# First MLP's loads behind the projections' weights, the output projection's behind the fifth pair's; the third block's statistics pinned

## The chip, the cores and the metric

The kernel runs on one core of a Trainium2 chip. The metric is the device time in microseconds of one launch; three runs of the kernel before gave 1535.03, 1537.14 and 1538.2, median 1537.14. One further execution was recorded by the hardware profiler: 1529.18 us, of which the instructions span 1527.5. All durations below are of that execution.

A core has five engines, each with an instruction queue of its own that it works off strictly in order: PE (TensorE, matrix products), DVE (VectorE), ACT (ScalarE), POOL (GpSimd) and SP (SyncE). SP issues nearly all loads of this kernel; ACT issues some stores. An instruction whose inputs aren't ready holds up everything behind it on its engine. A load is done some microseconds after its issue, and the same 16 DMA engines carry the loads of all issuers.

## The reference

One sequence of 2048 tokens with 512 features goes through a normalisation, a Mamba2 mixer with a gated MLP, another normalisation and a routed mixture of experts. Cut to what matters here:

```python
x = x + attn(layernorm(x))
x = x + ffn(layernorm(x))

def attn(hidden):
    h = hidden + mamba2(rmsnorm(hidden, ln1_w))
    h2 = rmsnorm(h, ln2_w)
    return h + (silu(h2 @ gate_w) * (h2 @ up_w)) @ down_w

def mamba2(x):
    z, xb, B, C, dt = split(x @ in_proj_w)         # 512 -> 2576
    xb, B, C = split(silu(conv(xb, B, C)))
    y = ssd_chunked(xb * softplus(dt + dt_bias), dt * A, B, C) + D * xb
    return rmsnorm(y * silu(z), norm_w) @ out_proj_w   # 1024 -> 512

def ffn(x):                                        # 8 experts, best 2 of each token
    w = top2(softmax(x @ Wr))
    return sum(w[e] * ((silu(x @ Wg[e]) * (x @ Wu[e])) @ Wd[e]))
```

All arithmetic is in float32.

## The kernel before

**Blocks.** The Mamba2 part works in eight blocks (b) of 256 tokens, each of two chunks of 128 tokens (t = 2b + j). The MLP works in four blocks (fb) of 512 tokens, that is two Mamba2 blocks, and in 16 chunks (c) of the 2048 inner features. The MLP of a block runs spread out between the Mamba2 steps of later blocks: `main` steps both generators in turn, the first MLP from within block 2 on. After all of it come routing and experts, which the change doesn't touch.

**The input projection.** Its weights are ten pairs of 512 KB (pairs 0 to 5: x, B and C; 6 to 9: the gate z), reloaded for each block. `load_w_in` (L96) loads one pair into a tile `wi` of a ring of three; the load of pair p + 2 is issued as pair p begins (`projected`, from L330). The products are `pm` (L340, for x, B and C; `pm_0` to `pm_5`) and `pz` (the gate, in the same function). Block 0's six pairs are projected in `main` ahead of everything else; those of block b + 1 and the gates of block b run between the pieces of chunk work of block b.

**Normalisation.** `prepare(b)` (L209) makes a block's statistics (`scales`, L190: bn_stats L149, bn_aggr L150, a square root on ACT, a reciprocal on DVE), the normalised rows `hn` (L219, one per chunk), and their transposes for the projection (PE L201, `hT` written by DVE L205). For block 1 an existing `issue_after` keeps it behind block 0's rows.

**Chunk work.** ACT, POOL and DVE make a chunk's decays: per-row sums of time steps are written out and read back spread over all partitions (`spread`, L305: loads `cum` of 512 KB each at L312, masked by POOL at L314; `ec` at L324), exponentiated by ACT (L420) and multiplied by DVE (L422). `xd` (L428) is the chunk's x times its time steps; PE's state product (L452) takes it. `dA` (L270) comes out of the time-step chain of a block, and PE's `pc` (L273) begins the block's sums with it. At a chunk's end the output product `po` (L490) multiplies the gated rows `zs` by the output projection `w_o` (1024 x 512, 2048 KB, loaded once at L878). Before that POOL multiplies the eight row groups of `w_o` by the norm's weights, in place (`weigh`, L888), during block 0.

**The MLP's products.** Instead of eight products of quarter blocks for gate and up together, a chunk does seven, with sums of weights and of activations. In the first MLP (fb = 0) the weights come as blocks (`load_early` L524: three loads of 128 KB into `mg`; `load_late` L537: one of 256 KB into `ms`) and POOL makes the sums (L531, L532, L542, L543); ACT then issues the stores of the finished tiles to memory (L544, L545), and later MLPs load those. `mg` and `ms` share a ring of three tiles. `load_down` (L550) loads a chunk's 256 KB of the down projection into `md`, a ring of four. PE's products of gate and up are at L780, their copies out of PSUM on ACT at L827, L834 and L821, and the gate product on POOL at L847.

**What sets the order.** A scheduler that weighs the program's instructions puts each engine's queue in order when the kernel is built. An instruction that nothing holds can land far ahead of its place in the program: the first MLP's loads, which only need free tiles, stand near the start of SP's queue, and the third block's first bn_stats near the start of DVE's. `tc.issue_after(x)` makes the instructions inside it come behind instruction x in that order. From block 2 on PE's order is fixed by the program; the other engines' is the scheduler's throughout. The order is the same in each execution.

Of the kernel before, what the change touches and what calls it, by code (L numbers as in the profile page):

```python
# [16 lines left out]
P = 128  # L17
# [37 lines left out]
def mamba_mlp_moe(ctx, tc, x, w_in, w_out, w_gu, w_down, par, wr, wr_rows, wg, wu, wd, out):  # L55
# [3 lines left out]
    nc = tc.nc  # L59
# [33 lines left out]
    w_in_k = w_in.rearrange("(k p) n -> p k n", p=P)  # L93
    nc.sync.dma_start(out=w_dt, in_=w_in_k[:, :, 2560:2576])

    def load_w_in(pair):  # L96

        w = pw.tile([P, NK, 2 * P], F32, name="wi", tag="wi", bufs=3)
        nc.sync.dma_start(out=w, in_=w_in_k[:, :, pair * 2 * P : (pair + 1) * 2 * P])
        return w  # L100

    ahead = [load_w_in(pair) for pair in range(2)]
# [102 lines left out]
            nc.vector.tensor_tensor(dst, pt, bc(weight, 2, P), ALU.mult)  # L205

    first_rows = None

    def prepare(b):  # L209

        nonlocal first_rows
        hT = wa.tile([P, NK, TB], F32, name=f"hT{b}", tag="hT")
        hns = []
        with tc.issue_after(first_rows) if b == 1 else ExitStack():
            scales(b)
            for j in range(NCH):
                t = b * NCH + j
                hns.append(wa.tile([P, D], F32, name=f"hn{t}", tag="tok", bufs=3))
                normed = nc.vector.tensor_scalar(  # L219
                    hns[j], res[t], mv[:, t, 0:1], rboth[:, t : t + 1], ALU.subtract, ALU.mult  # L220
                )
# [49 lines left out]
        n = NCH * NH  # L271
# [123 lines left out]
    def chunk(b, j, dt, ncum, dtdec, cd, cum, ec, xb, cs, zs):  # L395

        nonlocal summed
        t = b * NCH + j
        tok = slice(j * P, (j + 1) * P)
        halves = [slice(half * HD, (half + 1) * HD) for half in range(2)]  # L400
        sdt = sdiag[t % 2]
        xbt = xbts.pop(t)
        y = zs[:, :, tok]

        for gp in range(2):

            if t:
                with tc.issue_after(summed), tc.high_priority(AT_ONCE):
                    nc.gpsimd.tensor_tensor(ec[:, gp], ec[:, gp], cs[gp][:, :, tok], ALU.mult)

            psc = ps_sg.tile([P, 2, 4, P], F32, name=f"psc{t}_{gp}", tag="sg")
            for half in range(2):
                rows = halves[half]
                nc.tensor.matmul(psc[:, half], xb[rows, 2 + gp, tok], cs[gp][rows, :, tok], start=True, stop=True)  # L414


            lt = cum[gp].rearrange("p (a i) q -> p a i q", a=2)
            turns = [(half, i, 8 * gp + 4 * half + i) for i in range(4) for half in range(2)]
            for half, i, h in turns:
                nc.scalar.activation(lt[:, half, i], lt[:, half, i], AF.Exp, bias=ncum[:, j, h : h + 1])  # L420
            for half, i, h in turns:
                nc.vector.scalar_tensor_tensor(  # L422
                    lt[:, half, i], lt[:, half, i], dt[:, j, h : h + 1], psc[:, half, i], ALU.mult, ALU.mult
                )
            if gp == 0 and t < NT - 1:

                xd = wa.tile([P, 4, 4, HD], F32, name=f"xd{t}", tag="xd", bufs=1)
                nc.vector.tensor_tensor(  # L428
                    xd, bc(xbt[:, 0], 2, 4),
                    bc(dtdec[:, j, :].rearrange("p (g i) -> p g i", g=4), 3, HD), ALU.mult,  # L430
                )
            if gp:
                yield
            py = ps_y.tile([P, 4, P], F32, name=f"py{t}_{gp}", tag="y")
            if t:
                for i in range(4):
                    nc.tensor.matmul(
                        py[:, i, :], sdt[:, gp, i, :], ec[:, gp, i, :], start=(i == 0), stop=False,
                        skip_group_check=True,
                    )  # L440
            yield
            if gp == 0:
                yield
            for half in range(2):
                nc.tensor.matmul(
                    py[halves[half]], xbt[:, 0, 2 * gp + half, :], lt[:, half], start=not t, stop=True,
                    skip_group_check=True,
                )
            if gp == 0 and t < NT - 1:
                pst = ps_tr.tile([P, 2, 4, HD], F32, name=f"pst{t}", tag="tr")  # L450
                for g in range(4):
                    nc.tensor.matmul(pst[halves[g % 2], g // 2], xbt[:, 1, g, :], xd[:, g], start=True, stop=True)  # L452


            yd = wa.tile([P, 4, P], F32, name=f"yd{t}_{gp}", tag="y")
            for i in range(4):
                at = C_D + 4 * gp + i
                nc.vector.scalar_tensor_tensor(
                    yd[:, i, :], xb[:, gp, tok], params[:, at : at + 1], py[:, i, :], ALU.mult, ALU.add
                )  # L460
            nc.vector.tensor_tensor(y[:, 4 * gp : 4 * gp + 4, :], yd, y[:, 4 * gp : 4 * gp + 4, :], ALU.mult)

        if t < NT - 1:
            new = state
            if t:
                flat = state.rearrange("p g i d -> p (g i) d")
                nc.gpsimd.tensor_tensor(flat, flat, bc(cd[:, j].rearrange("p g i -> p (g i)"), 2, HD), ALU.mult)
                nc.vector.tensor_tensor(state, state, pst, ALU.add)
            else:
                nc.vector.tensor_copy(state, pst)  # L470
            nxt = sdiag[(t + 1) % 2]
            for half in range(2):
                nc.scalar.copy(nxt[halves[half], :, :, half * HD : (half + 1) * HD], new[halves[half]])

        yield
        if t < NT - 1:
            xbts[t + 1] = turned_x(t + 1, xb if j == 0 else xc[0])

        sq = wa.tile([P, 8, P], F32, name=f"sq{t}", tag="xd", bufs=1)
        with tc.high_priority(AT_ONCE):  # L480
            nc.scalar.activation(sq[:, 0:4, :], y[:, 0:4, :], AF.Square)
            nc.scalar.activation(sq[:, 4:8, :], y[:, 4:8, :], AF.Square)
            for n in (4, 2, 1):
                summed = nc.gpsimd.tensor_tensor(sq[:, 0:n, :], sq[:, 0:n, :], sq[:, n : 2 * n, :], ALU.add).ins
        yield


        po = ps_y.tile([P, D], F32, name=f"po{t}", tag="y") if t >= BPF * NCH else bank("g", [D], f"po{t}")
        for m in range(8):
            nc.tensor.matmul(po, y[:, m, :], w_o[:, m, :], start=(m == 0), stop=(m == 7))  # L490
        yield
        pms = ps_tr.tile([P, 1], F32, name=f"pms{t}", tag="tr")
        nc.tensor.matmul(pms, sq[:, 0, :], ones[:, 0:1], start=True, stop=True)

        ry = wa.tile([P, 1], F32, name=f"ry{t}", tag="ry")
        rsqrt_eps(ry, pms, scale=1.0 / DI)
        h = wa.tile([P, D], F32, name=f"h{t}", tag="tok", bufs=3)
        nc.vector.tensor_scalar(h, res[t], mv[:, t, 0:1], rstd[:, t : t + 1], ALU.subtract, ALU.mult)
        nc.vector.scalar_tensor_tensor(h, po, ry, h, ALU.mult, ALU.add)
        nc.gpsimd.tensor_tensor(res[t], res[t], h, ALU.add)  # L500
        nc.scalar.dma_start(out=resd[t], in_=res[t])

        m2 = wa.tile([P, 1], F32, name=f"m2{t}", tag="m2")
        nc.scalar.activation(sq[:, 4:8, :].rearrange("p a q -> p (a q)"), h, AF.Square, accum_out=m2)
        r2 = wa.tile([P, 1], F32, name=f"r2{t}", tag="r2")
        rsqrt_eps(r2, m2, scale=1.0 / D)
        nc.vector.tensor_scalar_mul(h, h, r2)
        yield
        fb, off = divmod(t * P, FB)
        if off == 0:  # L510
            h2T[fb] = (wk if fb % 2 else wa).tile([P, 2, NK, FH], F32, name=f"h2T{fb}", tag="h2T", bufs=1)
        half, off = divmod(off, FH)
        transposed(h, h2T[fb][:, half, :, off : off + P], params[:, C_L2 : C_L2 + NK])
# [36 lines left out]
    def load_down(c):  # L550
        d = pmlp.tile([P, D], F32, name="md", tag="md", bufs=4)
        nc.sync.dma_start(out=d, in_=w_down[c * FC : (c + 1) * FC, :])
        return d
# [213 lines left out]
    def feed_forward(fb):  # L767

        nonlocal mlp_w, newest, turning
        if fb == 0:  # L770
            w = load_early(0, 0)
            mlp_w = w, load_late(0, 0, w)
        b11, b21, b22, t1, t2, t3, t4 = sums(fb)
        rows = []
# [13 lines left out]
        for c in range(NFC):  # L788
# [59 lines left out]
            if pair:  # L848
                mlp_down(fb, rows, 2 * (c % 2) + 1, pair)
            newest = a.rearrange("p h q -> p (h q)")  # L850
            made[c] = newest, load_down(c)
            if more:
                early, late = coming
            yield
# [15 lines left out]
    ready = None  # L870
    for pair in range(6):
        finish(project(0, pair, hT, *xc))
        if pair < 2:
            next(coming)
        elif pair == 2:
            ready = finish(coming)
            near = [spread(0, 0, ready[-1])]
    nc.sync.dma_start(out=w_o, in_=w_out.rearrange("(t p) n -> p t n", p=P))  # L878
    near.append(spread(0, 1, ready[-1]))
    xbts[0] = turned_x(0, xc[0])  # L880

# [390 lines left out]
```

## Time and profile before

| | |
|---|---|
| Runs | 1535.03, 1537.14, 1538.2 us |
| Profiled execution / its span | 1529.18 / 1527.5 us |
| Granted PE clock, mean | 0.994 |
| PE, DVE, ACT, POOL busy | 97%, 53%, 47%, 28% |
| First loads of `mg`, `ms`, `md` issued | 11.29 to 23.82 us |
| `w_o` issued | 6.52 us |
| Third to fifth `wi` issued | 5.27, 15.31, 20.97 us |
| Sixth and seventh `wi` issued (one entry) | 27.59 us |
| First `pm_5` matmul | 34.48 us |
| First use of `w_o` (POOL, L888) | 57.74 us |
| First output product begins / ends | 71.48 / 80.29 us |
| First MLP product on PE | 222.15 us |

Such a profile is read from the busiest engine: with PE at 97%, a stretch in which PE waits counts, and a busier DVE or ACT counts only where PE waits for it. For every group of instructions the page gives busy time, the mean length of one in nanoseconds, and after the second bar the time in which the engine stood idle just before, with what ended the wait. A float32 matmul is recorded as two, so the sixteen records of `pm` that stand together are one pair. The timeline gives the start of each run of equal instructions and, in brackets, the idle time ahead of it. The windows give the granted clock of PE, where 1.00 is full speed.

### The profile page before, as it was taken

The numbers are of one execution on the slowest core, as the hardware profiler recorded it, in microseconds if no ns is written. First come the engines' busy times: TensorE is split into PE (matmuls) and PEld (weight loads), VectorE is DVE, ScalarE is ACT, GpSimd is POOL, SyncE is SP. The second block draws the span as 40 slices with busy tenths as digits, with TensorE's granted clock in tenths as the row PEclk, the third lists the DMA queues.
The fourth block names the chain that finished last, engine by engine and source line by source line (L and its number), as shares of the span: only waits on it lengthen the run. The fifth ranks groups of instructions, "written<-read, shape, count | busy, mean of one in ns | idle before, by whom it ended". The sixth has DMA issues, their size and how long they took to land. (4 is left out here: it accounts for less than half of the span.)

```text
span 1527.5 us, 18831 instructions
## 1 busy us (share of the span) xinstructions
PE 1483.2 (97%) x6009; PEld 1006.8 (66%) x6009; DVE 812.5 (53%) x2119; ACT 723.7 (47%) x1309; POOL 430.5 (28%) x537
## 2 busy tenths in 40 slices
PE   8899999999999999999999999998999999999996
PEld 7656577677667676767676667665776666656653
DVE  7776875645555565657645764555343445322221
ACT  5887966735663578458745653232221122111110
POOL 3442324423242212121233121113121123533321
PEclk9999999999999999999999999999999999999998
DMA  9443445644554655656347554438879643443332
GB/s 306 133 145 118 145 135 184 197 145 162 165 177 149 224 167 176 192 166 210 125 105 246 173 168 139 165 121 206 270 222 253 202 116 67 55 75 69 63 62 36
DMA packets 138899, 238.00 MB, mean 156 GB/s; under 512 B 13744, under 2 KB 74032, under 8 KB 138800
## 3 DMA queue, kind: packets, MB, share of 16 engines
q1 hardware_dynamic: 116032, 186.79, 40.1%
q0 software_dynamic: 9088, 18.91, 7.3%
q10 hardware_dynamic: 13680, 31.07, 5.4%
q8 instruction: 51, 0.84, 0.2%
q14 instruction: 48, 0.39, 0.1%
HBM read 195.93 MB, written 40.80 MB: 155 GB/s over the span
## 5 line engine op out<-in xcount | busy, mean ns | idle before, releaser
L764 PE MATMUL pd<-md,a 128*128 128x512 f32 x512 | 238.8, 593 | 1.4 <-DVE r L765 0.9
L340 PE MATMUL pm<-hT,wi 128*128 128x256 f32 x768 | 185.3, 386 | 3.4 <-DMA wi<-in_w_in 3.4
L340 PEld LDWEIGHTS pm<-hT,wi 128*128 128x128 f32 x768 | 141.9, 192 | 28.6 <-issue 10.8
L765 DVE TENSOR_TENSOR r<-r,pd 128x512 f32<-128x512 f32 x128 | 87.5, 684 | 136.0 <-PE pd L764 132.7
L764 PEld LDWEIGHTS pd<-md,a 128*128 128x128 f32 x512 | 97.2, 190 | 76.4 <-issue 64.6
L361 DVE SCALAR_TENSOR_TENSOR ca<-pre,params,ca 128x256 f32<-128x256 f32 x288 | 141.7, 549 | 0.3
L780 PE MATMUL py<-h2T,ms 128*128 128x256 f32 x512 | 131.7, 380 | 2.0 <-DMA ms<-late 2.0
L340 PE MATMUL pz<-hT,wi 128*128 128x256 f32 x512 | 117.0, 381 | 0.0
L490 PE MATMUL po<-w_o,zs 128*128 128x512 f32 x256 | 114.5, 600 | 0.0
L847 POOL TENSOR_TENSOR a<-a,up 128x256 f32<-128x256 f32 x64 | 48.1, 752 | 230.3 <-DVE up L841 184.6
L1121 PE MATMUL epg<-ew,xgT 128*128 x288 | 109.0, 460 | 0.2 <-ACT xgT L203 0.2
L1121 PE MATMUL epu<-ew,xgT 128*128 x288 | 108.7, 459 | 0.0
L780 PEld LDWEIGHTS py<-h2T,ms 128*128 128x128 f32 x512 | 95.5, 190 | 17.8 <-issue 2.9
L340 PEld LDWEIGHTS pz<-hT,wi 128*128 128x128 f32 x512 | 94.9, 190 | 13.7 <-issue 0.8
L1143 PE MATMUL epd<-ew,ehT 128*128 (+1 forms) x216 | 99.0, 594 | 1.0 <-DVE ehT L1136 1.0
L420 ACT ACT_TABLE_LOAD x68 | 87.2, 1283 | 22.8 <-DMA xnd<-xn 8.4
L420 ACT ACTIVATE cum<-cum,ncum 128x128 f32<-128x128 f32 x256 | 84.6, 391 | 7.3 <-POOL cum L314 6.3
L490 PEld LDWEIGHTS po<-w_o,zs 128*128 128x128 f32 x256 | 49.1, 193 | 57.8 <-issue 56.5
L827 ACT COPY a<-px 128x256 f32<-128x256 f32 x64 | 23.6, 369 | 127.0 <-PE px L780 115.6
L1101 POOL DMA_INDIRECT xg<-xnd,idx x36 | 35.5, 985 | 157.7 <-PE pt L201 150.8
L314 POOL TENSOR_SCALAR_AFFINE_SELECT cum<-cum 128x1024 f32<-128x1024 f32 x32 | 36.2, 1131 | 151.0 <-DMA cum<-rowsd 140.7
L422 DVE SCALAR_TENSOR_TENSOR cum<-cum,dt,psc 128x128 f32<-128x128 f32 x256 | 72.2, 339 | 5.1 <-PE psc L414 2.8
(247 smaller groups left out, 2550.7 us busy)
## 6 DMA issues: line engine op xcount, KB each, us to landing
wi<-in_w_in SPq DMA_DIRECT2D x80, 512.0 KB, 3.9
ms<-late SPq DMA_DIRECT2D x48, 512.0 KB, 4.4
mg<-early SPq DMA_DIRECT2D x48, 384.0 KB, 3.9
md<-in_w_down SPq DMA_DIRECT2D x64, 256.0 KB, 4.3
cum<-rowsd SPq DMA_DIRECT2D x32, 512.0 KB, 4.3
col<-in_wr_rows SPq DMA_DIRECT2D x64, 256.0 KB, 3.9
late<-ms ACTq DMA_DIRECT2D x16, 512.0 KB, 2.6
ec<-rowsd SPq DMA_DIRECT2D x60, 128.0 KB, 4.0
```

Source lines behind the costliest of these rows:

```text
L314: nc.gpsimd.affine_select(out=c, in_=c, pattern=[[0, 8], [1, P]], compare_op=ALU.is_ge, fill=-3.0e38, base=0, channel_multiplier=-1,)
L340: nc.tensor.matmul(pm[:, m, :], w[:, k, m * P : (m + 1) * P], hT[:, k, :], start=(k == 0), stop=(k == NK - 1))
L361: nc.vector.scalar_tensor_tensor(ca, pre[:, m, k : k + TB], cw[:, k : k + 1], ca, ALU.mult, ALU.add)
L420: nc.scalar.activation(lt[:, half, i], lt[:, half, i], AF.Exp, bias=ncum[:, j, h : h + 1])
L422: nc.vector.scalar_tensor_tensor(lt[:, half, i], lt[:, half, i], dt[:, j, h : h + 1], psc[:, half, i], ALU.mult, ALU.mult)
L490: nc.tensor.matmul(po, y[:, m, :], w_o[:, m, :], start=(m == 0), stop=(m == 7))
L764: nc.tensor.matmul(pd, a[:, j * P : (j + 1) * P], d, start=(m == 0), stop=(m == 1))
L765: turning = nc.vector.tensor_tensor(rows[j], rows[j], pd, ALU.add).ins
L780: nc.tensor.matmul(ps, w[:, k], m[:, k], start=(first and k == 0), stop=(k == KH - 1), skip_group_check=True)
L847: nc.gpsimd.tensor_tensor(a[:, 1], a[:, 1], up, ALU.mult)
L1121: nc.tensor.matmul(ps, xT[:, k, :], w[:, lo : lo + EI], start=(k == 0), stop=(k == NK - 1))
L1143: nc.tensor.matmul(pd, hT[:n, m, :], w[:n, NG + m * D : NG + (m + 1) * D], start=(m == 0), stop=(m == len(ET) - 1))
```

## The change

`load_w_in` remembers the load it issued last in `loaded`. The first MLP's loads of `mg`, `ms` and `md` are built inside `issue_after(loaded)`, so they come behind the projection weights that had been asked for last when the program reached them: in the built order SP issues the first of them behind a `wi` load near the end of block 3's projection (217.11 us in the profile before). The load of `w_o` moves into the loop over block 0's pairs, behind the load that the pair with index 2 asked for: that of the fifth pair (index 4). And `prepare(2)`, the third block's statistics and normalised rows, comes behind `xd` of chunk 1.

```diff
+    loaded = None
+
     def load_w_in(pair):
+        nonlocal loaded
         w = pw.tile([P, NK, 2 * P], F32, name="wi", tag="wi", bufs=3)
-        nc.sync.dma_start(out=w, in_=w_in_k[:, :, pair * 2 * P : (pair + 1) * 2 * P])
+        loaded = nc.sync.dma_start(out=w, in_=w_in_k[:, :, pair * 2 * P : (pair + 1) * 2 * P]).ins
         return w
...
     first_rows = None
+    xds = {}
 
     def prepare(b):
...
-        with tc.issue_after(first_rows) if b == 1 else ExitStack():
+        with tc.issue_after(first_rows if b == 1 else xds[1]) if b in (1, 2) else ExitStack():
             scales(b)
...
-                nc.vector.tensor_tensor(
+                xds[t] = nc.vector.tensor_tensor(
                     xd, bc(xbt[:, 0], 2, 4),
                     bc(dtdec[:, j, :].rearrange("p (g i) -> p g i", g=4), 3, HD), ALU.mult,
-                )
+                ).ins
...
         if fb == 0:
-            w = load_early(0, 0)
+            with tc.issue_after(loaded):
+                w = load_early(0, 0)
             mlp_w = w, load_late(0, 0, w)
...
-            made[c] = newest, load_down(c)
+            with ExitStack() if fb else tc.issue_after(loaded):
+                made[c] = newest, load_down(c)
...
         if pair == 2:
+            with tc.issue_after(loaded):
+                nc.sync.dma_start(out=w_o, in_=w_out.rearrange("(t p) n -> p t n", p=P))
...
-    nc.sync.dma_start(out=w_o, in_=w_out.rearrange("(t p) n -> p t n", p=P))
```

PE's own order is the same in both from 222 us on; before that some transposes and products of blocks 0 and 1 change places.

More of the change, by code (lines that the diff above doesn't have):

```diff
@@ L872, in mamba_mlp_moe @@
         finish(project(0, pair, hT, *xc))
+        if pair == 2:
+            with tc.issue_after(loaded):
+                nc.sync.dma_start(out=w_o, in_=w_out.rearrange("(t p) n -> p t n", p=P))
         if pair < 2:
```

## The prediction

> **What bounds the kernel.** I read the page's head first, then the 40 slices, then the groups with the idle time before them.
>
> ```profile
> PE 1483.2 (97%) x6009; PEld 1006.8 (66%) x6009; DVE 812.5 (53%) x2119; ACT 723.7 (47%) x1309; POOL 430.5 (28%) x537
> PE   8899999999999999999999999998999999999996
> L340 PE MATMUL pm<-hT,wi 128*128 128x256 f32 x768 | 185.3, 386 | 3.4 <-DMA wi<-in_w_in 3.4
> L490 PE MATMUL po<-w_o,zs 128*128 128x512 f32 x256 | 114.5, 600 | 0.0
> ```
>
> TensorE is busy 97% of the span. Work that the change moves on other engines is worth what it does to PE's idle time, and to PE's clock after an idle stretch. PE's waits over the whole run add up to some 30 us, 15.6 of them in the first 180 us. The largest single one is the 3.4 us on the third row: the sixth projection (pm_5) waits for its weights. The timeline around it and around the next long wait:
>
> ```profile
> 34.48 5.22 PE L340 MATMUL pm<-hT,wi 128*128 128x256 f32 x16 [3.39 <-DMA wi<-in_w_in]
> 70.64 0.38 PE L273 MATMUL pc<-tri,dA 128*32 128x128 f32 x2 [2.93 <-DVE dA L270]
> 71.48 8.81 PE L490 MATMUL po<-w_o,zs 128*128 128x512 f32 x16
> 237.29 7.03 PE L490 MATMUL po<-w_o,zs 128*128 128x512 f32 x16
> ```
>
> Start, length, what ran, and in brackets the idle time before it. The same sixteen matmuls take 3.70 us at 218.62 and 5.22 after the wait; the output product takes 7.03 at 237 and 8.81 behind the second wait. So each of these two waits cost its own length and 1.5 to 1.8 us of slow matmuls. By stretches (columns: length, busy of PE, PEld, DVE, ACT, POOL, granted clock, DMA share, GB/s):
>
> ```profile
> 10.00:20.00 10.00, 9.61 (x51) 8.37 (x52) 7.05 (x31) 2.50 (x6) 0.64 (x3) 1.00 1.05 396
> 34.00:36.00 2.00, 1.51 (x4) 1.28 (x5) 1.86 (x5) 1.96 (x4) 0.61 (x3) 0.54 1.04 398
> 72.00:75.00 3.00, 3.00 (x5) 1.35 (x4) 2.62 (x6) 3.00 (x11) 2.67 (x4) 0.50 0.56 134
> ```
>
> Until 36 us the DMA engines are full (396 to 398 GB/s); that is the only stage bound by transfers. The clock is 0.50 to 0.54 after the two waits.
>
> **A rule weighed.** The Trainium skill, "TensorE: Matmul & The Clock Gate", Part 1, says that the clock halves after about one idle window of some 3.4 us, free-running, and comes back after as much work. The rows: 0.54 after 3.39 us idle, 0.50 after 2.93, and no slowing after a wait of 2.02 at 151.01. By the rule a wait under 3.4 us costs only itself; by the rows one of 2.9 us costs 1.8 more. I take the rows: the bound lies between 2.0 and 2.9 us.
>
> **Part 1: the first MLP's loads leave the start (a gain).** Five loads of gate and up weights' blocks of 128 KB and one more, ms of 256 KB and md of 256 KB stand between 11.29 and 23.82 in SP's queue: 6 x 128 + 512 = 1.25 MB, at 396 GB/s 3.3 us. Their six additions on POOL (22.4 to 28.3, 4.73 us) go too. Beside them the DVE's convolution steps took 3.08 us for four where four take 1.65 at 200.74; over that stretch I estimate 2.8 us of DVE time saved.
>
> **Part 2: w_o moves behind the fourth and fifth pairs' loads.** Before it is issued at 6.52 (2 MB, 5.3 us at 396 GB/s); now at about 22, and the two cum loads (1 MB) and the sixth pair's wi (0.5 MB) stand behind it. So 3.5 MB must pass from about 21 to 22.6 us on: 8.8 us at 396 GB/s, 12.9 at the 271 GB/s of the 20 to 30 us stretch (cum loads ran in it). The sixth wi would land at 30 to 35.5; I take 33.2, against 34.4 before. Thus the stall is **not** removed by w_o's move: it takes the place of the small loads. But in the built order PE does two more of the x transposes and block 1's first four hn transposes ahead of pm_5 (0.38 us for two at 30.72, 0.60 for four at 200.38: some 0.8 to 1.0), which stood behind it before; the idle stretch is cut up, and I expect the clock to hold: 1.6 us. Summed at this point: 1.1 + 0.8 + 1.6 = 3.5.
>
> ScalarE follows: it stood idle for 3.03 us at 39.80 waiting for pm_5 and is then busy without a gap until 67. That gap closes, so the time-step chain (u at 61.53 before) comes at about 59, and dA, for which PE waits 2.93 at 70.64, at 66.4 to 67.9. POOL's last two row scalings of w_o stood at 77.38 and now come at about 73, since the order puts the first projection of block 1 wholly before pc. End of the output product: 80.29 before, 74 to 77 now by this chain, that is 3.3 to 6. w_o itself lands by 32 and its first use is POOL's at 57.74: its delay is covered by 25 us. PE idles 7.4 us between 71 and 222 before, so most of the gain is carried. **Gain taken: 4.5 us, ends 1 and 6** (1 where the sixth wi is as late as before and the clock drops still).
>
> **Part 3: the third block's statistics.** bn_stats and aggregate (0.69 + 0.16 us) of its first tile leave the start, which is in the gain. The price is later: VectorE's order at 195–205 us is changed for the following block too.
>
> ```profile
> 200.38 0.60 PE L201 MATMUL pt<-ident,hn 128*128 128x128 f32 x4
> 205.10 0.66 PE L201 MATMUL pt<-ident,hn 128*128 128x128 f32 x4 [0.66 <-DVE hT L205]
> 207.30 0.66 PE L201 MATMUL pt<-ident,h 128*128 128x128 f32 x4 [1.55 <-DVE hT L205]
> ```
>
> The normalised rows hn6 and hn7 (1.98 us at 195.91) are ready before PE asks at 200.38. In the built order of the changed kernel they stand behind eight decay products (2 us), xd (1.21) and one h (0.5 to 0.9) on VectorE: ready near 202.8, so PE waits 2.5 to 3.1 us; of the 2.2 us of waits that follow, most goes, since VectorE has then done what they wait for. **Loss taken: 1.7, ends 0 and 3.** Three ACT table loads of 1.28 us are saved around block 1; ScalarE isn't what PE waits for there, so nothing.
>
> **Part 4: the first MLP starts with its weights just loaded (a loss).** The loads are issued behind the last but one projection weight of block 3, at 217.11 before. Ordering: three mg, md, ms, three mg, rowsd and so on. Issue 217.5 to 220.4, landing 3.9 us later (page, mg row): 221.3 to 224. The first product wants mg at 222.15: no more than 0.5. POOL then adds 1, 2 (0.98 + 0.79) for mg, needed as early[:,2] at 223.9: ready at 224.0 to 224.3, 0 to 0.5.
>
> What costs more is ScalarE, which issues the saved copies of the sums:
>
> ```profile
> 239.07 0.35 ACTq L544 DMA_DIRECT2D early<-mg  x1
> 239.47 0.37 ACT L834 COPY a<-px 128x256 f32<-128x256 f32 x1 [3.33 <-POOL mg L532]
> ```
>
> The trigger waits for POOL's additions, and the copy queued behind it waits 3.33 us with it. Before, this trigger of the third chunk's sums is behind the second chunk's first copy (234.91); in the changed order it stands **ahead** of it. POOL has before those additions: the late sums of the second chunk (ready at 231, as the ms load waits for a buffer that an earlier saved copy, 2.6 us, must free), three squares (2.5), two ec products (2.55), a gate product (0.72), the two additions (1.77). 231 + 7.5 = 238.5; then trigger and copy end at 239.3. The second product into the same bank on PE needs that copy: at 235.57 before, now up to 3.7 us later; what PE can do first is only the 0.9 us between. I take 2.9 to 3.7 for this wait, a clock drop of 1.6 half the time, and 0.2 for the two small ones: **4.3, ends 0** (POOL earlier than I count) **and 6.**
>
> Rule against this part: "DMA: Bandwidth & Descriptors", Rules for kernel authors, says to issue a DMA early and wait late. By it the load time of 3.9 us would be exposed at 222; by the rows of issue only 0 to 0.5 of it is, as the issue is still 4.6 us ahead of use. I take the rows.
>
> **Sum.** −4.5 + 1.7 + 4.3 = +1.5 us against the profiled execution's 1529.18 (span 1527.5 and 1.7 around it); that execution lies 8 us under the median of the runs, 1537.14, to which I add the difference: 1538.6. About 0.2%, 3.07 us, is what separates from no change here; +1.5 is within it.
>
> **Rivals.**
> - A, the forecast: gain and losses nearly cancel, −1.6 to +4.6. Chance 0.38.
> - B, faster: the start gains in full (6), and the trigger is released early, since POOL idles 7.3 us before 225.85 and is only 28% busy; block 3's wait is eaten by waits there anyway. −6 + 0.5 + 0.5 = −5: 1532. For it: the start's waits are the largest in the profile, and what follows is slack in the page's busy shares. Against: the order on ScalarE is fixed. Chance 0.27.
> - C, slower: ScalarE's trigger ahead of the copy, one mechanism at 235–239 us. It decides from the point where POOL's sums come more than 2.9 us after PE's want, when the clock drops with it: 3.7 + 1.6 + up to 1 for the following up copy = 6.3; with 1.7 and a start gain of only 3, +5: 1542. For it: the 3.33 us wait in the row above is the same mechanism. Chance 0.30.
> - D, the change doesn't do what it says at the start: w_o and the cum loads keep pm_5 as late as 34.4, the clock drops, gain 1: with both losses +5 as well, 1542; told from C at 34 us. Chance 0.05, in with C.
>
> **Chances and range.** Faster than 1534.07: B and none of A's: 0.27. Within: A, 0.34. Slower than 1540.2: C, D and A's upper end, 0.39. Range: from B's 1532 down one, to 1531, and from C's 1542 up by the 3 us that its unknown ends leave, 1545; the likeliest's own is 1535.5 to 1541.7.
>
> **What would show it.** At 31–35 us: a wait for wi of about 2 us, not 3.4, clock near 1 at 34–38. At 66–71 us: the dA wait; the output product ends before 78. At 200–205: PE waits for hn. At 235–239: ACT's trigger ahead of the copy with a POOL wait, and PE idle some 3 us. Wrong if the start gains over 6 us, or if no wait over 1 us stands at 222–240.

## The result, and the profile after

The changed kernel is slower: 20 runs with a median of 1540.81 us against 1533.57 for 20 runs of the kernel before beside them, ratio 1.0034 with a 95% interval of 1.0022 to 1.0046, that is 5.2 us (3.4 to 7.1; the two medians lie 7.2 apart). The profiled execution spans 1533.3 us against 1527.5, 5.8 more. The changed kernel's 20 runs go from 1532.7 to 1546.1 with the granted clock: the eight with a mean of 0.993 or more took at most 1537.1, the twelve with 0.991 or less at least 1539.7, and the profiled one, at 1535.1, is one of the eight. Two groups of the page of the changed kernel answer to those shown of before (line numbers are up to eight higher):

```profile
PE 1484.7 (97%) x6009; PEld 1006.1 (66%) x6009; DVE 802.0 (52%) x2119; ACT 724.0 (47%) x1310; POOL 430.4 (28%) x537
L344 PE MATMUL pm<-hT,wi 128*128 128x256 f32 x768 | 186.7, 389 | 2.3 <-DMA wi<-in_w_in 2.3
L494 PE MATMUL po<-w_o,zs 128*128 128x512 f32 x256 | 113.3, 593 | 2.3 <-POOL w_o L896 2.3
```

PE is busy 1.5 us longer (1484.7 against 1483.2), so most of the 5.8 us is in waits. The wait for the sixth pair's weights is down from 3.4 to 2.3, and a new one of 2.3 for a row group of w_o that POOL scales has come. Where the rest lies is seen by setting equal points of PE's work side by side in the two timelines:

| PE reaches | before, us | after, us | after minus before |
|---|---|---|---|
| `pn` of block 1 | 80.22 | 77.97 | −2.25 |
| `pn` of block 2 | 158.39 | 154.51 | −3.88 |
| `py<-ec` of block 2's second chunk | 195.93 | 193.81 | −2.12 |
| first MLP product | 222.15 | 222.28 | +0.13 |
| output product after it | 237.29 | 244.06 | +6.77 |
| `pn` of block 3 | 244.26 | 251.02 | +6.76 |
| end of span | 1527.5 | 1533.3 | +5.8 |

So 3.9 us are won by 158 us, 1.8 lost by 195, 2.2 more by 222, and 6.6 within 15 us at the first MLP's start. From 244 us to the end the distance shrinks by 1.0. The waits at those places, from PE's timeline of the changed kernel (start, length, what, and the idle time ahead of it with its releaser):

```profile
35.96 5.22 PE L344 MATMUL pm<-hT,wi 128*128 128x256 f32 x16 [2.31 <-DMA wi<-in_w_in]
68.04 0.38 PE L277 MATMUL pc<-tri,dA 128*32 128x128 f32 x2 [1.39 <-DVE dA L274]
76.91 1.12 PE L494 MATMUL po<-w_o,zs 128*128 128x512 f32 x2 [2.29 <-POOL w_o L896]
...
202.08 0.63 PE L204 MATMUL pt<-ident,hn 128*128 128x128 f32 x4 [3.65 <-ACT zs L377]
209.07 0.66 PE L204 MATMUL pt<-ident,h 128*128 128x128 f32 x4 [0.78 <-DVE hT L208]
...
227.75 1.13 PE L785 MATMUL py<-ts,mg 128*128 128x256 f32 x4 [2.27 <-DVE a L813]
236.60 0.41 PE L277 MATMUL pc<-tri,dA 128*32 128x128 f32 x2 [1.76 <-ACT xbt L393]
242.07 1.10 PE L785 MATMUL px<-ts,mg 128*128 128x256 f32 x4 [1.41 <-ACT a L832]
```

The last three are 5.4 us of waits where the kernel before waited for nothing. What stands behind the first of them is on VectorE and POOL. VectorE of the kernel before, and below it VectorE and POOL of the changed one:

```profile
222.17 1.55 DVE L261 SCALAR_TENSOR_TENSOR acc<-acc,s 128x32 f32<-128x32 f32 x7
224.15 0.42 DVE L808 TENSOR_TENSOR a<-a,py 128x256 f32<-128x256 f32 x1 [0.43 <-PE py L780]
```

```profile
223.68 3.46 DVE L265 SCALAR_TENSOR_TENSOR acc<-acc,s 128x32 f32<-128x32 f32 x7
227.28 0.41 DVE L813 TENSOR_TENSOR a<-a,py 128x256 f32<-128x256 f32 x1
```

```profile
222.20 0.73 POOL L535 TENSOR_TENSOR mg<-mg 128x256 f32<-128x256 f32 x1 [3.00 <-DMA mg<-in_w_gu]
225.92 0.72 POOL L536 TENSOR_TENSOR mg<-mg 128x256 f32<-128x256 f32 x1
```

The seven acc steps of the time-step chain are the same instructions; they take 1.55 us before and 3.46 after, 0.22 and 0.49 each. The difference is POOL: its six sums of the MLP's weights run from 222.20 to 226.64, beside them. The Trainium skill, "GPSIMD Engine Reference", 8. Key points, says that POOL shares its SBUF interfaces with VectorE and contends with VectorE's instructions that have two SBUF inputs, as the acc steps have; it gives no size there, the trace does: 2.2 times in all. The steps aren't slowed evenly, though. One of POOL's sums and a step that begins beside it:

```profile
223.57 0.73 POOL L536 TENSOR_TENSOR mg<-mg 128x256 f32<-128x256 f32 x1
223.68 0.66 DVE L265 SCALAR_TENSOR_TENSOR acc<-acc,s 128x32 f32<-128x32 f32 x1
```

The sum ends at 224.30 and the step at 224.34. The other three steps that begin in the midst of a sum also end about 0.05 us behind it; one that begins together with a sum takes its usual 0.19. So the price of such a step is the rest of POOL's instruction, not a fixed factor. The addition to `a` that PE waits for stands behind the seven steps on VectorE in both kernels.

### The profile page after: what moved, and what is told of

It reads as the page before. It is cut to its first block, busy times and chain, and to the rows that moved or that the text cites. A ratio compares the mean times of both kernels' runs of the same rounds, so it can differ in the third digit from the quotient of the medians.

```text
span 1533.3 us, 18840 instructions
## 1 busy us (share of the span) xinstructions
PE 1484.7 (97%) x6009; PEld 1006.1 (66%) x6009; DVE 802.0 (52%) x2119; ACT 724.0 (47%) x1310; POOL 430.4 (28%) x537
## 3 DMA queue, kind: packets, MB, share of 16 engines
q0 software_dynamic: 9088, 18.91, 7.3%
HBM read 195.93 MB, written 40.80 MB: 154 GB/s over the span
## 5 line engine op out<-in xcount | busy, mean ns | idle before, releaser
L344 PEld LDWEIGHTS pm<-hT,wi 128*128 128x128 f32 x768 | 143.0, 193 | 28.7 <-issue 8.4
L365 DVE SCALAR_TENSOR_TENSOR ca<-pre,params,ca 128x256 f32<-128x256 f32 x288 | 131.9, 515 | 0.2
L1129 PEld LDWEIGHTS epu<-ew,xgT 128*128 128x128 f32 x288 | 54.7, 190 | 30.5
```

What stands on the lines that cost most here:

```text
L344: nc.tensor.matmul(pm[:, m, :], w[:, k, m * P : (m + 1) * P], hT[:, k, :], start=(k == 0), stop=(k == NK - 1))
L365: nc.vector.scalar_tensor_tensor(ca, pre[:, m, k : k + TB], cw[:, k : k + 1], ca, ALU.mult, ALU.add)
L1129: nc.tensor.matmul(ps, xT[:, k, :], w[:, lo : lo + EI], start=(k == 0), stop=(k == NK - 1))
```

## The experiments

Each kernel was timed against the kernel before on the same chip, in four sessions; the kernel before had medians of 1533.6, 1540.1, 1535.0 and 1538.9 us in them, so times are compared by ratio within a session. "MLP way" is the time on PE's timeline from the first MLP product to the output product behind it (15.14 us before, 21.78 after); the expectations from no_hold to early4_hn count to the end of that output product, 7 us more (22 and 28.7). "Start" is PE's distance to the kernel before at `pn` of block 2 (158.39 us there).

### One part undone at a time

**no_hold**: the MLP's loads free.

```diff
-            with tc.issue_after(loaded):
-                w = load_early(0, 0)
+            w = load_early(0, 0)
...
-            with ExitStack() if fb else tc.issue_after(loaded):
-                made[c] = newest, load_down(c)
+            made[c] = newest, load_down(c)
```

> The changed kernel with the first MLP's loads free again (they return to the start of SP's queue); w_o behind the fifth pair's load and the pin stay. Theory H (the hold costs, by the first MLP's start at 222 to 251 us, where the changed kernel lost 6.6 us): the 6.6 us go, the first MLP's PE work from its first product to the end of the output product takes about 22 us as before and not 28.7; the start keeps part of its gain; ratio to before 0.997 to 1.000. Rival W (w_o's move or the pin costs): ratio stays at 1.003.

Measured: ratio 1.0060 (1.0036 to 1.0084), above the changed kernel's 1.0034 (the intervals overlap), where I expected faster. With the loads free, SP issues four `md` and all six gate and up blocks from 8.31 to 17.6 us, ahead of the fourth `wi`, and w_o only at 23.14. PE is 6.3 us behind already at `pn` of block 0 (3.4 of it a wait for dA), waits 3.4 us for the scaled w_o at 85.31, and is 7.3 behind at 158 us. So w_o's move without the hold is worse than the kernel before. The MLP way is 20.97 us, not 15: the store described under held_b0 is ahead of the copy here too, and the clock is 0.50 at 247 to 251 us behind that wait. The wait of 3.65 us near 200 us is gone (0.39 and 2.34 stand there, 0.66 and 1.55 in the kernel before), which says that it is the hold that brings it.

**no_wo**: w_o's load at its old line.

```diff
-        if pair == 2:
-            with tc.issue_after(loaded):
-                nc.sync.dma_start(out=w_o, in_=w_out.rearrange("(t p) n -> p t n", p=P))
...
+    nc.sync.dma_start(out=w_o, in_=w_out.rearrange("(t p) n -> p t n", p=P))
     near.append(spread(0, 1, ready[-1]))
```

> The changed kernel with w_o's load back behind the third wi; hold and pin stay. Theory H: still slower than before, ratio 1.002 to 1.005, with the 28.7 us at the first MLP's start; the sixth pair's weights land earlier than in the changed kernel (w_o is no longer ahead of them), so that PE's wait for wi near 34 us is under 1 us and the start gains 2 us more than the changed kernel's 2.2. Rival W: ratio 1.000 or below.

Measured: ratio 1.0022 (1.0011 to 1.0033). PE waits for `wi` nowhere in the run, and the start is −4.37, the best of all profiles. The place of w_o is what kept pm_5 late in the changed kernel. The MLP way is 24.54 us, some of it at a clock of 0.50 to 0.54 from 228 to 234 us, so the loss there isn't w_o's.

**no_pin**: the third block's statistics free.

```diff
-        with tc.issue_after(first_rows if b == 1 else xds[1]) if b in (1, 2) else ExitStack():
+        with tc.issue_after(first_rows) if b == 1 else ExitStack():
```

> The changed kernel without the pin of the third block's statistics. My prediction put the loss at 195 to 205 us (PE waiting for the fourth block's normalised rows) on the pin. Theory P: without it that wait (3.65 us) is gone and the ratio falls by 0.0015. Rival: the built order at that place is the same without the pin, so the wait of 3 to 4 us stays and the ratio is that of the changed kernel, 1.003, give or take 0.001.

Measured: ratio 1.0088 (1.0067 to 1.0109), the slowest of all and far above both expectations. The wait of 3.65 us near 200 us stays, so my prediction had put it on the wrong part. What the pin does is elsewhere. VectorE and PE of this kernel:

```profile
14.54 0.69 DVE L152 BATCH_NORM_STATS2 bn<-x 128x6 f32<-128x512 f32 x1 [6.05 <-DMA x<-in_x]
15.15 1.27 DVE L208 TENSOR_TENSOR hT<-pt,params 128x512 f32<-128x512 f32 x2
```

```profile
15.87 3.59 PE L243 MATMUL pdt<-w_dt,hT 128*128 128x16 f32 x16 [7.60 <-DVE hT L208]
```

The third block's bn_stats stands ahead of block 0's `hT` on VectorE and waits 6.05 us for its x, whose load comes late behind the weights; PE waits 7.60 us for that `hT`. Without the pin the new order of loads is ruined at once.

**held_b0**: the hold ends earlier, behind the last load that block 0's loop asks for.

```diff
+    held = loaded
     near.append(spread(0, 1, ready[-1]))
...
-            with tc.issue_after(loaded):
+            with tc.issue_after(held):
                 w = load_early(0, 0)
...
-            with ExitStack() if fb else tc.issue_after(loaded):
+            with ExitStack() if fb else tc.issue_after(held):
```

> The changed kernel with the first MLP's loads behind the last projection weights asked for in block 0's loop (some 30 to 45 us) instead of behind those of block 3. Theory H (what costs is that loads and sums come as late as the first product): the first MLP's start takes 22 to 25 us again, the start's gain stays, only the wait near 200 us (3.65) remains; ratio 0.997 to 1.001. Rival W: 1.003 as the changed kernel.

Measured: ratio 1.0051 (1.0033 to 1.0069) with seven runs, above what was expected. The MLP way is 18.77 us: POOL makes no sums near 222 us and the acc steps are fast (six in 1.32 us), yet 3.6 us remain. They are one wait and its surroundings:

```profile
241.78 1.13 PE L785 MATMUL px<-ts,mg 128*128 128x256 f32 x4 [2.68 <-ACT a L832]
```

It is the product behind ScalarE's copy that stands behind the store of the third chunk's sums, as in my prediction's part 4. The profiled execution, 1541.2 us, is the fastest of the seven (median 1546.5), so what makes the others slower isn't seen in it and stays open.

### The two mechanisms at the MLP's start, apart

**pool_alone**: the kernel before, with POOL work alone. The orders of the other four engines are unchanged; the additions change no output.

```diff
+    filler = wa.tile([P, 200], F32, name="filler", bufs=1)
+    nc.gpsimd.memset(filler, 0.0)
...
-                nc.gpsimd.tensor_tensor(flat, flat, bc(cd[:, j].rearrange("p g i -> p (g i)"), 2, HD), ALU.mult)
+                scaled = nc.gpsimd.tensor_tensor(flat, flat, bc(cd[:, j].rearrange("p g i -> p (g i)"), 2, HD), ALU.mult).ins
+                if t == 5:
+                    with tc.issue_after(scaled), tc.high_priority(AT_ONCE):
+                        for _ in range(11):
+                            nc.gpsimd.tensor_tensor(filler, filler, filler, ALU.add)
```

> The kernel before with eleven POOL additions of 128x200 on a spare tile behind the state product that ends at 218.5 us, and nothing else; every other engine's order is unchanged. Theory K (POOL's additions slow VectorE's small operations beside them, and the first MLP's addition stands behind these): the seven acc steps of the time-step chain take 3.4 to 4.0 us instead of 1.55, PE waits 1.5 to 2.5 us for VectorE's addition to a ahead of its fourth MLP product, where it waited for nothing before, and the end of the output product comes 2 to 4 us later. Rival L (what was late in the changed kernel is the load of the weights): acc steps 1.55 us, no wait, ratio 1.000.

```profile
223.77 2.35 DVE L261 SCALAR_TENSOR_TENSOR acc<-acc,s 128x32 f32<-128x32 f32 x7
```

```profile
224.19 0.58 POOL L473 TENSOR_TENSOR filler<-filler 128x200 f32<-128x200 f32 x1
224.42 0.40 DVE L261 SCALAR_TENSOR_TENSOR acc<-acc,s 128x32 f32<-128x32 f32 x1
```

```profile
224.78 1.13 PE L786 MATMUL px<-ts,mg 128*128 128x256 f32 x4 [0.99 <-ACT a L833]
226.51 1.13 PE L786 MATMUL py<-ts,mg 128*128 128x256 f32 x4 [0.60 <-DVE a L814]
```

Measured: ratio 1.0017 (1.0005 to 1.0028), 2.6 us. The acc steps take 2.35 us, less than expected: an addition of 200 columns takes 0.58 us, and a step that begins beside it ends just behind it, as in the changed kernel. PE waits 0.60 us for the addition to `a`, where it waited for nothing. The MLP way is 17.27 us, 2.1 more than before, but the 0.99 us for ScalarE's copy is not POOL's. early4, with no sums beside its acc steps, has the same wait (0.98): in both, ScalarE's last copy of the state (`sdiag`) ends 3.1 us ahead of the first MLP product, in the kernel before 4.7, and from there to the copy ScalarE takes 5.55 us in both. PE was sooner there, for in the kernel before its clock was low at 208 to 212 us (see the last section). No load was moved, so rival L falls for the slow steps: POOL's work alone makes them. The size doesn't come with it: 0.6 us of wait are a quarter of the changed kernel's 2.27, and the rest of the 2.6 us stays open.

**early4**: the changed kernel with the hold three projection loads earlier, so that the sums run from about 200 us on, where POOL is idle.

```diff
+            held = loads[-4]
-            with tc.issue_after(loaded):
+            with tc.issue_after(held):
                 w = load_early(0, 0)
```

(`loads` collects what `load_w_in` issues.)

> The changed kernel with the first MLP's first loads behind the projection load three before the one they stand behind there, so that POOL's six sums run some 10 us earlier, where POOL is idle; in the built order ScalarE's store of the third chunk's sums then stands behind the second chunk's first copy, as in the kernel before. Theory K with my prediction's part 4 (contention and that store make the loss): the acc steps take 1.55 us, and the way from the first MLP product to the end of the output product is 22 to 24 us, not 28.7. The wait near 200 us stays or grows by 1. Ratio 0.999 to 1.001. Rival (some other cost of the hold): 27 us or more, 1.003.

```profile
230.15 1.55 DVE L267 SCALAR_TENSOR_TENSOR acc<-acc,s 128x32 f32<-128x32 f32 x7
```

Measured: ratio 1.0010 (0.9998 to 1.0021). The acc steps are back at 1.55 us and PE doesn't wait for the addition to `a`, and in this order the store is behind the copy. The MLP way is 16.42 us, 5.4 less than in the changed kernel. The price moved: the sums now run beside the normalisation of block 3, and the wait near 200 us has grown from 3.65 to 4.66. In all profiles together, PE waits 1.65 to 2.32 us for the addition to `a` in the six with the first MLP's sums beside the acc steps (after, after_again, no_wo, no_pin, hn_fix, store_fix), and not at all in the seven with no POOL work there.

**hn_fix**: block 3's rows back in their old place on VectorE.

```diff
-        with tc.issue_after(first_rows if b == 1 else xds[1]) if b in (1, 2) else ExitStack():
+        with ExitStack() as pins:
+            if b in (1, 2):
+                pins.enter_context(tc.issue_after(first_rows if b == 1 else xds[1]))
+            elif b == 3:
+                pins.enter_context(tc.issue_after(convs[2, 9]))
+                pins.enter_context(tc.high_priority(AT_ONCE))
             scales(b)
```

(`convs` keeps the last convolution step of each group of channels.)

> The changed kernel with block 3's statistics and normalised rows put behind the same convolution step of VectorE as in the kernel before. Theory N (the wait of 3.65 us near 200 us and the slow clock after it come from these rows' place in VectorE's order): the wait is gone or under 1 us, PE reaches the first MLP product 2 to 4 us earlier against the kernel before than the changed kernel does; the loss of 5 to 7 us at the first MLP's start stays; ratio 1.000 to 1.002. Rival (the profile's releaser, ScalarE's zs, holds PE): the wait stays.

Measured: ratio 1.0023 (1.0012 to 1.0035). The wait of 3.65 us is gone though the page had named ScalarE's zs as its releaser; 0.23 and 1.92 stand in its place. From 158 us to the first MLP product PE loses 0.9 us against the kernel before, where the changed kernel loses 4.0; from the second chunk's `py<-ec` on it takes 26.17 us, before 26.22 and the changed kernel 28.47. The expected gain at 222 us isn't there: its start is +0.27 instead of −3.88, though nothing in its order differs ahead of block 3's rows (from 125 us on). That is taken up below.

**early4_hn**: both.

> Both: the earlier hold and block 3's rows in their old place. In this built order the store of the third chunk's sums stands ahead of the second chunk's first copy again. If the parts add: start's gain 2 to 4 kept, no wait near 200, first MLP's start 22 to 25 us: ratio 0.997 to 1.000, faster than both kernels. If the store alone costs 2.7 to 3 us as in held_b0: 1.000 to 1.001.

Measured: ratio 1.0031 (1.0020 to 1.0042). The MLP way is 19.18 us with a wait of 3.08 for the copy behind the store: the parts add only as far as the scheduler leaves each order alone, and here it put the store ahead again. The sums beside block 3's normalisation also cost 2.64 and 1.68 us of waits for `hT`.

**store_fix**: the changed kernel with the third chunk's store behind the second chunk's first copy.

```diff
-            nc.scalar.dma_start(out=early_d[c], in_=w[:, 0:3])
-            nc.scalar.dma_start(out=late_d[c], in_=v)
+            with tc.issue_after(copied) if c == 2 else ExitStack():
+                nc.scalar.dma_start(out=early_d[c], in_=w[:, 0:3])
+                nc.scalar.dma_start(out=late_d[c], in_=v)
...
-                nc.scalar.copy(a[:, 0], x1)
+                copied = nc.scalar.copy(a[:, 0], x1).ins
```

> The changed kernel with one order changed: the store of the third chunk's sums on ScalarE comes behind the second chunk's first copy; in the built order nothing differs ahead of 222 us. If the store ahead of the copy costs 2.5 to 4 us (as the runs with it and without POOL's sums beside it show: 18.8 and 19.2 us from the first MLP product to the output product, against 15.1 before) and POOL's sums the rest, that way takes 17.5 to 19 us instead of 21.8, and the ratio falls from 1.0034 to 1.001 to 1.002. Rival (the store only hides behind a wait that stays): 21 to 22 us and 1.003.

Measured: ratio 1.0024 (1.0013 to 1.0035); MLP way 20.46 us, only 1.3 less. The wait of 1.41 for the first copy is gone and one of 0.87 for the copy `up`, which still stands behind the store, has come. The size that I expected was missed. I read it so that where the sums are late as well, a part of the store's cost hides behind their waits; the run undoes only one of the two copies, so it doesn't show how much. Set together (the way takes in slow clocks where they fall in it, at no_hold, no_wo, no_pin and hn_fix):

| MLP way, us | store behind both copies | store ahead of a copy |
|---|---|---|
| no sums beside the acc steps | before 15.14, held_all_wo 15.74, early4 16.42 | held_b0 18.77, held_all 18.91, early4_hn 19.18, no_hold 20.97 |
| sums (or filler) beside them | pool_alone 17.27 (filler) | store_fix 20.46, after 21.78 and 21.71, hn_fix 22.34, no_pin 23.25, no_wo 24.54 |

### A version without what was found, and the changed kernel again

**held_all**: held_b0 with hn_fix and store_fix. **held_all_wo**: the same with w_o's load at its old line.

> w_o behind the fifth pair, pin, first MLP's loads behind block 0's last projection load, block 3's rows in their old place on VectorE, and the store behind the copy: each mechanism found is taken out. If they add: from 151 to 222 us a loss of 1 to 2 us against the kernel before, from the first MLP product to the output product 15 to 16.5 us, the start as the changed kernel's, a mean gain of 1 to 2: ratio 0.998 to 1.001. If something else of the change costs: above 1.002.

> As held_all, but w_o's load at its old place behind the third wi. The one run with w_o early and the small loads held had the shortest start (PE 4.4 us ahead of the kernel before at 158 us): if that is w_o's place, ratio 0.996 to 0.999, faster than both kernels; if it was the clock in that one execution, the same as held_all, 0.998 to 1.001.

Measured: held_all 1.0011 (0.9996 to 1.0025), held_all_wo 0.9986 (0.9975 to 0.9996). The second is faster than both kernels, 2.2 us below the one before. Its group of projections waits for no weights:

```profile
L350 PE MATMUL pm<-hT,wi 128*128 128x256 f32 x768 | 183.8, 385 | 0.0
```

Before it was 3.4 us and in the changed kernel 2.3. Its start is −3.42 and its MLP way 15.74. In held_all PE waits 7.2 us for scaled row groups of w_o (4.0 the longest) and 2.69 for a copy behind the store; its profiled execution is the slowest of its 14. The store stands behind both copies in the one and ahead of one in the other, so the two differ in more than w_o.

**after_again**: the changed kernel unchanged.

> The changed kernel once more. Its order of instructions up to 190 us is the same as in hn_fix and early4, which stood 0.3 us behind the kernel before at 158 us, where the changed kernel's profiled execution was 3.9 us ahead. Theory C (how long the clock stays low after the two waits of the start differs from execution to execution): at 158 us this one lies anywhere from 4 ahead to 1 behind, with the same instructions and another clock at 34 to 40 and 70 to 75 us; the way from the first MLP product to the output product is 21 to 24.5 us again. Rival (hn_fix and early4 moved something early that the built order does not show): 3.9 ahead again.

Measured: ratio 1.0036 (1.0024 to 1.0048), MLP way 21.71, and a start of −1.07 instead of −3.88. This execution spans 1546.3 us, 13.0 more than the first: 2.9 of them stand at `pn` of block 3, the other 10 come later, where among other things its waits for `ms` are 6.8 us against 1.4. No run here looks into those. Window rows of the first profile, then of this one (length, busy of PE, PEld, DVE, ACT, POOL, granted clock, DMA share, GB/s):

```profile
36.00:38.00 2.00, 2.00 (x5) 1.65 (x6) 2.00 (x4) 1.18 (x3) 0.19 (x1) 0.50 1.06 408
72.00:75.00 3.00, 2.62 (x7) 0.84 (x5) 0.96 (x2) 2.98 (x4) 3.00 (x4) 1.00 0.90 292
```

```profile
36.00:38.00 2.00, 1.56 (x7) 1.41 (x8) 2.00 (x3) 1.31 (x2) 0.30 (x1) 1.00 1.08 402
72.00:75.00 3.00, 3.00 (x5) 1.13 (x4) 1.74 (x5) 3.00 (x8) 3.00 (x2) 0.50 0.56 173
```

The same wait for the same load (2.31 and 2.29 us) is followed by a clock of 0.50 in one execution and 1.00 in the other; the one with the fast clock there then waits 4.28 us for dA instead of 1.39, since VectorE's chain comes no earlier, and has the slow clock behind that. The six profiles that share the changed kernel's early order have starts of −3.88, −1.07, −1.30, −1.43, +0.27 and +0.33, mean −1.2; the two with the order of before 0 and +1.39. So about 1.9 us of gain is what repeats, as far as eight profiles tell, and the profile of the changed kernel showed it at its best. The profiles come from three sessions, so a part of the spread may be the chips'.

## Where the prediction was right and where it failed

The time fell in the range and the loss was at the place that was looked at, but the forecast itself, no change, was wrong: the measured +5.2 us is rival C's +5. That this number came so near is in good part luck. C's own mechanism, the trigger ahead of the copy, made 1.41 us of wait, and three terms that C didn't have (POOL's sums beside VectorE, a late store and the split pairs) made most of the rest. And the base of 1537.14, from three runs, lies 3.6 us above the 1533.57 of the 20 runs beside the changed kernel, so that the time is nearer to the forecast than the difference is. Of D its sign came (pm_5 as late as 35.96, clock 0.50), but not its small gain.

- **The start, taken at 4.5 us.** The mechanism was right in that w_o takes the small loads' place, and wrong in how much is left: the sixth pair's weights let PE go on at 35.96, not at 33.2, later than the 34.48 before. "I expect the clock to hold: 1.6 us" was a coin that fell on the wrong side in the profile (0.50) and on the right one in after_again. dA came nearly as predicted (PE at 68.04 against 66.4 to 67.9). POOL's last scalings did not come at 73: PE waited 2.29 us for one at 76.91, a wait that I hadn't foreseen, and the output product ended at 78.0 and not between 74 and 77. Measured: 2.25 at 80 us, 3.9 at 158, about 1.9 in the mean of the executions.
- **A term that was missing: split pairs.** "Most of the gain is carried" fails between 158 and 195 us, where 1.8 us go without a wait to name. The scores `psc` use half of the array's rows each and `py<-cum` half of its columns. PE's timeline before, then after:

```profile
162.88 1.13 PE L414 MATMUL psc<-cs,xb 64*128 64x512 f32 x4
169.01 1.08 PE L445 MATMUL py<-cum,xbt 128*64 128x512 f32 x4
```

```profile
158.56 1.12 PE L418 MATMUL psc<-cs,xb 64*128 64x512 f32 x2
160.17 1.12 PE L418 MATMUL psc<-cs,xb 64*128 64x512 f32 x2
165.77 1.07 PE L449 MATMUL py<-cum,xbt 128*64 128x512 f32 x2
167.36 1.07 PE L449 MATMUL py<-cum,xbt 128*64 128x512 f32 x2
```

  Two half-size products side by side take 1.1 us together; with another instruction between them each takes that alone. The new order splits one pair of each kind, both in block 2's first chunk (PE's order changes up to 190 us, not in blocks 0 and 1 alone): some 2 us. The Trainium skill, "TensorE: Matmul & The Clock Gate", Part 3, says that matmuls on different tiles of the array run at the same time; the rows agree, and show what that needs. PE's busy time in this stretch is 35.8 us in the two profiles that split neither pair (before, pool_alone) and 37.6 to 37.9 in the ten that split both there. No run puts the two pairs together again and changes nothing else, so this cause rests on rows and comparison.
- **Part 3, taken at 1.7 (0 to 3).** Measured 2.2 from 195 to 222 us: right in mechanism and size, wrong in the cause. It is not the pin (no_pin keeps the wait) but the hold (no_hold has none), which changes where VectorE's order puts these rows; hn_fix, which puts them back, shows that their place is all of it. The pin itself has a gain that the sum didn't have: 7.6 us at the start, which the moved loads would cost without it.
- **Part 4, taken at 4.3 (0 to 6).** Measured 6.6. The landing and the first sum were right: early[:,2] was ready at 224.30 and PE waited 0.18. The store was right as a mechanism: 

```profile
241.19 0.33 ACTq L548 DMA_DIRECT2D early<-mg  x1
241.56 0.37 ACT L832 COPY a<-px 128x256 f32<-128x256 f32 x1 [3.09 <-POOL pre L357]
```

  held_b0 and early4_hn show it without the sums beside, 2.68 and 3.08 us of wait against the 2.9 to 3.7 taken. In the changed kernel itself it is 1.41, since PE is already late. The term that is missing is POOL's sums beside VectorE: I credited the start with 2.8 us for the same contention and left it out where the sums went to. It costs 2.27 us at once. The 1.76 us at pc come by another way, also missing. SP's queue of the kernel before, and of the changed one with what it waited for:

```profile
225.80 0.60 SPq L541 DMA_DIRECT2D ms<-in_w_gu  x1
```

```profile
229.61 0.57 SPq L545 DMA_DIRECT2D ms<-in_w_gu  x1
SPq L545 <- DMA early<-mg: 6.0, 1, 6.0
```

  The next ms load needs the tile of the first chunk's `mg`. Before, PE's last product of it frees it. Now the store of its sums, triggered at 224.33, must land too: that takes 5.2 us, and PE's last product of the tile has ended at 228.88, 0.6 us earlier. Behind this load stand POOL's sum, ScalarE's trigger of its store and the copy `xbt`, for which pc waits. No run here takes this store away alone.
- **The bound for the clock, put between 2.0 and 2.9 us.** The trace of before shows that it doesn't hold: behind the waits of 0.66 and 1.55 us in the prediction's own rows at 205 to 207 the clock is 0.56, and a `py<-cum` group that else takes 1.08 us takes 1.66. The last section has the row.
- **The rule on early issue** (DMA early, wait late) I set aside by the rows, and for the load itself that held: 0.18 us. What it cost was the work that follows the load, the sums and the stores, and that did come too late.

Of the sum −4.5 + 1.7 + 4.3, the gain was some 0.6 too large against the profile and 2.6 against the mean, the losses were 4.6 too small: 2.3 in part 4, 0.5 in part 3, 1.8 in the missing term. On the profile's own numbers −3.9 + 1.8 + 2.2 + 6.6 = +6.7, of which 1.0 comes back later.

## What to carry to other kernels

A load that is moved takes its consumers along: price the additions, the stores and the buffers that follow it at their new place, on every engine that they run beside, with the same contention that is credited at the old one. Where a scheduler sets the order, the pins matter as much as the move: read the built order of every engine at each place where PE has little slack, and look there for halves of the array that are no longer neighbours and for a DMA trigger ahead of a copy. A gain that consists of a clock that didn't drop is to be taken at half, or not at all: it came in one of two executions here.

## What was not expected of the hardware

A wait of 2.3 us on PE, 0.82 us of another wait ahead of it, was followed by a clock of 0.50 in one execution and of 1.00 in the next of the same kernel, and in the first of the two the wait of 2.29 us that ends at 76.91 was followed by 1.00. No length of wait divides these: in the kernel before the clock held behind 2.02 us and fell behind 0.66 and 1.55. Its window there:

```profile
208.00:210.00 2.00, 2.00 (x8) 0.76 (x10) 1.79 (x4) 1.99 (x5) 0.51 (x1) 0.56 0.03 8
```

The Trainium skill, "TensorE: Matmul & The Clock Gate", Part 1, says that the window is free-running and the penalty varies from run to run; these rows are what that looks like, at shorter waits than the 3.4 us that it names. And a VectorE step with a single input slows down too beside POOL's sums: acc's first step (L263), 128x32, took 0.64 us against 0.18.
